# Respaced steps, a norm on another engine and a scheduling priority in a two-layer perceiver kernel

## The chip, the core and the metric

The kernel runs on one core of a Trainium2 chip. The metric is the device time of one launch in microseconds (us), as the median of repeated runs. The engines are named as the profile names them: PE (TensorE, matrix products), DVE (VectorE), ACT (ScalarE), POOL (GpSimd) and SP (SyncE, which issues most DMAs).

## The reference

The input is x, 64 sequences of 32 tokens with 256 features, and a context of 257 rows for each sequence. All is float32. There are two layers of three blocks, each added to x after a layer norm of x without weights:

```
x = x + cross_attn_0(context, norm(x), mask)   # 16 heads of 64; both sides layer-normed with g, b;
                                               # q and k rms-normed per head; keys = context + own tokens
x = x + self_attn_0(norm(x))                   # 16 heads of 16, q and k rms-normed
x = x + moe(norm(x))                           # 64 experts, top 8, 128 slots each, and a shared expert
x = x + cross_attn_1(norm(x), context)         # 16 heads of 64, plain softmax
x = x + self_attn_1(norm(x))                   # latent, rotary, causal
x = x + tanh((h W) A1 A2 + bias)               # h = norm(x)
```

The context's norm of the first block is the part that the change moves to another engine: `(cx - mean) * rstd * g + b` on 256 of the 257 rows of each context.

## The kernel before

**Tiles.** The 2048 tokens lie in 16 tiles `t` of 128 tokens; a tile holds four sequences, so there are 64 contexts `s = 4t + b`. The run has four stages: the first layer's cross-attention, with its self-attention and the routing threaded in (`before`); the experts (`experts`); the second layer (`after`); and drains in which the last tiles' steps run with nothing beside them.

**Who orders what.** PE executes exactly the order in which the Python code issues its instructions (`manual_schedule`). For all other engines a list scheduler orders the instructions: among those that it takes to be ready it picks the one with the lowest priority number, which is by default its place in the program. `nc.any` operations go to DVE or ACT as the scheduler chooses. PSUM has eight banks, all taken from one pool by `bank`.

**The first loop.** For each context `s` the body of the loop in `before` issues, in this order:

1. `keys(s+2)`: eight products `psA<-xT,wk` (L167, called at L195), their copies to `kT` by turns on ACT (L1201) and DVE (L1203), and after each four of them one squaring `sq` on ACT (L1206).
2. `weigh(s)`: the transposes of the attention weights (L207) and the copies `at` (L208).
3. slot 1.
4. `norms(s+2)`: eight small products of `sq` (L1218), `values(s)` (L221, L231, copies L233), `spread(s+2)` (L1239, exponentials L1240 on ACT).
5. slot 2.
6. `turn(s+3)` (transposes L1173, copy `xT` L1176), `scores(s+2)` (L1258, the multiplication L1267 out of PSUM on DVE, the softmax of L176 to L197 on DVE and ACT), `prepare(s+4)` (the context's norm).
7. slot 3, or, for the last context of a tile, the start of a tail.

A *slot* advances every live generator by one step, that is, up to its next `yield`. There are two kinds. A *front* is `CrossFirst.queries(t+1)`: norm, transposes, the query products, and the query transposes L1135. A *tail* is `tail(t)`: the output products (`heads_out`: `yT,wv`, then `wo,oT` at L258), the self-attention (`self_first`, `attend_self` with L310), and the routing (`route`). A tile has eleven slots, numbered i0 to i10 here: three in each context and two in the last. A `yield` with nothing before it moves later steps to later slots. So the placing of the yields decides which products of PE stand between a product of the main chain and the next one that needs its copy.

**The second loop.** In `after` the body is: `scores(s+2)`, slot A, `weigh(s)` (transposes L1375, copies `at` L1376), slot B, `values(s)`, slot C. The generators are `CrossSecond.queries(t+2)` and `follow(t)` (`heads_out`, `self_second`, `ffn`).

**The experts.** PE works through 64 experts, with the weights `we` fetched `AHEAD` = 12 experts ahead. After expert 12 `after_weights` loads and folds the second layer's weights; it ends with `latent_weights` and `ffn_weights`, whose scratch pools share memory.

Of the kernel before, what the change touches and what calls it, by code (L numbers as in the profile page):

```python
# [41 lines left out]
PLACES = (0, 2, 1, 3), (1, 3, 0, 2)  # L42

# [42 lines left out]

def done(steps):
    for _ in steps:
        pass


class Kernel:
# [7 lines left out]


# [50 lines left out]
    def normed(self, t):  # L152

        z = self.wk.tile([P, 1, D], F32, name="z")
        self.layernorm(z, self.x[:, t : t + 1, :])
        yield
        if self.slack:
            yield
        zT = self.wk.tile([P, 2, P], F32, name="zT")
        self.transposed(zT, z[:, 0, :])  # L160
        yield
        return z, zT
# [6 lines left out]
    def add_to_x(self, t, ps, bias=None):  # L169
        nc, xt = self.nc, self.x[:, t, :]  # L170
        if bias is not None:
            nc.gpsimd.tensor_tensor(xt, xt, bias, ALU.add)
        nc.vector.tensor_tensor(xt, xt, ps, ALU.add)
# [63 lines left out]
    def heads_out(self, t, yT, wv, wo, bias, split=False):  # L237
# [18 lines left out]
        yield  # L256
        ps = self.bank("psY")
        self.product(ps[:, :D], [oT[:, p, :] for p in range(8)], [wo[:, p, :] for p in range(8)])  # L258
        self.add_to_x(t, ps[:, :D], bias)
# [31 lines left out]
    def attend_self(self, t, e, recip, wo, bias):  # L291
# [6 lines left out]
        yield  # L298
        if self.slack:
            yield  # L300
# [71 lines left out]
    def before(self, ctx):  # L372


        self.eb, self.vb, self.slack = 1, 2, False
# [44 lines left out]
        next(first)  # L420
        next(first)
        cross.prepare(1)
        for i in range(2):
            cross.load(i + 2)
            cross.turn(i)
            cross.keys(i)
            cross.norms(i)
            done(first)
            cross.spread(i)
            cross.scores(i)  # L430
        cross.load(4)
        cross.prepare(2)
        cross.prepare(3)
        cross.turn(2)
# [47 lines left out]
        for s in range(n):  # L482
# [8 lines left out]
            if s + 2 < n:  # L491
                cross.keys(s + 2)
            cross.weigh(s)
            slot()
            if s + 2 < n:
                cross.norms(s + 2)
            cross.values(s)
            if s + 2 < n:
                cross.spread(s + 2)
            slot()  # L500
            if s + 3 < n:
                cross.turn(s + 3)
# [13 lines left out]
    def tail(self, t, yT, wv, wo, bo, sw, swo, sg, gw):  # L516

        yield from self.heads_out(t, yT, wv, wo, bo, True)
        yield
        if t == self.nt - 2:  # L520

            for _ in range(HOLD):
                yield
# [3 lines left out]
    def self_first(self, t, sw, swo, sg):  # L527
        nc = self.nc
        _, zT = yield from self.normed(t)
# [12 lines left out]
        )  # L542
        ps = self.bank("psA")
# [42 lines left out]
        yield from self.attend_self(t, e, recip, swo, None)  # L586

    def route(self, t, gw):
# [30 lines left out]

        yield  # L620
# [35 lines left out]
    def experts(self, ctx, slot, tails):  # L656
# [94 lines left out]
        for e in range(E):  # L751
# [8 lines left out]
            if e == AHEAD:  # L760
                self.after_weights()
        done(side)
# [34 lines left out]
    def after_weights(self):  # L797
# [8 lines left out]
        self.ffnw = self.ffn_weights(w)  # L806

    def after(self, ctx):
        self.eb = self.vb = 1
        self.slack = True  # L810
# [26 lines left out]
        for s in range(n):  # L837
# [3 lines left out]
            if s + 2 < n:  # L841
                cross.scores(s + 2)
# [5 lines left out]
            cross.weigh(s)  # L848
# [5 lines left out]
            cross.values(s)  # L854
# [115 lines left out]
    def self_second(self, t, wl, bl, wvo, bvo, wqk, bqk, wo, bo):  # L970
        nc = self.nc
        _, zT = yield from self.normed(t)
# [44 lines left out]
        yield  # L1017

# [25 lines left out]
        yield from self.attend_self(t, e, recip, wo, bo)  # L1044
# [18 lines left out]
    def ffn(self, t, m, bias):  # L1063
        nc = self.nc
        _, zT = yield from self.normed(t)
# [13 lines left out]
class CrossFirst:  # L1079
# [11 lines left out]
    def queries(self, t):  # L1091
# [8 lines left out]
        yield  # L1100
        lnT = k.wkx.tile([P, 2, P], F32, name="lnT")
# [7 lines left out]
        for n in range(2):  # L1109
# [10 lines left out]
            )  # L1120
        nc.vector.tensor_scalar(ss, ss, float(DH) * 1e-16, None, ALU.max)
# [34 lines left out]
    def prepare(self, s):  # L1156

        k, nc, cx = self.k, self.k.nc, self.cx[s]
        k.layernorm(cx, cx)
        nc.gpsimd.tensor_tensor(cx, cx, self.gx.unsqueeze(1).to_broadcast([P, 2, D]), ALU.mult)  # L1160
        nc.gpsimd.tensor_tensor(cx, cx, self.bx.unsqueeze(1).to_broadcast([P, 2, D]), ALU.add)
# [81 lines left out]
    def scores(self, s):  # L1243
# [6 lines left out]
        for half in range(2):  # L1250
# [14 lines left out]
            for i in range(2):  # L1265
                g = 2 * half + i
                nc.vector.tensor_tensor(sim[:, g, :], ps[i][:, :JK], sim[:, g, :], ALU.mult)  # L1267
# [18 lines left out]
class CrossSecond:  # L1286
# [7 lines left out]
    def queries(self, t):  # L1294

        k, nc = self.k, self.k.nc
        _, zT = yield from k.normed(t)
# [174 lines left out]
```

## Time and profile before

| | us |
|---|---|
| median of 3 runs | 2828.25 (2827.0 to 2829.42) |
| the profiled execution, own time | 2804.67 |
| its span, first to last instruction | 2802.8 |
| PE busy in the span | 2657.6 |
| DVE busy | 1694.9 |
| ACT busy | 1241.6 |
| POOL busy | 684.3 |

The profiled execution is 23.6 us (0.8%) under the median of the runs. A sum of durations from its trace is therefore set against its 2804.67 us, and carried over to the median in proportion.

How to read it: the end of a matrix product is modelled, so a product that waits in the middle of a group can look busy. In the timeline the first column is the start of a group and the second its modelled length. The distance from one group's start to the next group's start is what PE spent on the group, waits included. Groups of one kind are compared by that distance.

### The profile page before, as it was taken

What the parts mean: (1) busy time and instruction counts of PE and PEld (TensorE: products, weight loads), DVE (VectorE), ACT (ScalarE), POOL (GpSimd) and SP (SyncE); (2) the same over time, 40 slices, a digit from 0 to 9 for tenths busy, and PEclk for the clock granted to TensorE, in tenths of its full rate; (3) what the DMA queues carried; (4) which work ended last, traced back from release to release, by engine and by line L of the source; (5) the groups of instructions that cost most, each with busy time, mean ns of one, the idle gap of its engine ahead of it and who ended that gap; (6) DMA issues with size and microseconds to landing.
All of it is one profiled execution on the core that took longest, in us unless ns stands there. A gap on an engine that the chain in (4) does not pass through costs nothing. (4 is left out here: it accounts for less than half of the span.)

```text
span 2802.8 us, 58905 instructions
## 1 busy us (share of the span) xinstructions
PE 2657.6 (95%) x23386; PEld 1824.5 (65%) x23386; DVE 1694.9 (60%) x4427; ACT 1241.6 (44%) x3436; POOL 684.3 (24%) x756
## 2 busy tenths in 40 slices
PE   6999999999999999999999799999999999999996
PEld 3556666666666666666666578667777777777764
DVE  5546666666666666666665433466666666666664
ACT  3455555555555555555554223333333333333331
POOL 5211333133313331243121200321212222121001
PEclk8999999999999999999999899999999999999997
DMA  8000011011000000000001677321211222222110
GB/s 271 16 14 18 31 33 31 18 31 33 29 18 27 26 22 18 20 19 16 18 7 38 233 237 243 91 67 54 58 51 50 59 52 58 56 51 55 33 35 5
DMA packets 136087, 157.03 MB, mean 56 GB/s; under 512 B 24024, under 2 KB 118979, under 8 KB 135812
## 3 DMA queue, kind: packets, MB, share of 16 engines
q1 hardware_dynamic: 114308, 119.65, 13.8%
q0 software_dynamic: 12288, 25.21, 3.4%
q10 hardware_dynamic: 9216, 8.39, 0.9%
q8 instruction: 185, 3.03, 0.4%
q14 instruction: 90, 0.74, 0.1%
HBM read 121.63 MB, written 37.75 MB: 57 GB/s over the span
## 5 line engine op out<-in xcount | busy, mean ns | idle before, releaser
L167 PE MATMUL psA<-xT,wk 128*128 128x289 f32 x2048 | 517.4, 411 | 7.9 <-ACT xT L1176 4.5
L167 PEld LDWEIGHTS psA<-xT,wk 128*128 128x128 f32 x2048 | 388.0, 191 | 134.8 <-issue 21.8
L780 POOL DMA_INDIRECT y<-oute,idx x128 | 131.5, 1028 | 643.4 <-DVE x L791 453.9
L167 PE MATMUL psA<-at,cx 128*128 128x512 f32 x512 | 235.4, 602 | 20.0 <-ACT qTl L1005 18.2
L221 PE MATMUL psY<-at,cx 128*128 128x512 f32 x512 | 239.8, 612 | 0.1
L167 PE MATMUL psY<-xT,qk 128*128 128x257 f32 x1024 | 234.3, 382 | 0.0
L167 PEld LDWEIGHTS psY<-xT,qk 128*128 128x128 f32 x1024 | 190.8, 190 | 35.0 <-issue 10.2
L1357 DVE TENSOR_REDUCE mx<-psY 128x1 f32<-128x257 f32 x256 | 105.7, 423 | 133.6 <-PE psY L167 133.5
L1358 ACT ACTIVATE sim<-psY,mx 128x257 f32<-128x257 f32 x256 | 121.6, 476 | 142.3 <-DVE mx L1357 142.2
L184 ACT ACTIVATE sim<-sim,mx 128x289 f32<-128x289 f32 x256 | 134.1, 526 | 100.0 <-DVE mx L182 100.0
L221 PEld LDWEIGHTS psY<-at,cx 128*128 128x128 f32 x512 | 93.5, 192 | 123.0 <-issue 108.8
L167 PEld LDWEIGHTS psA<-at,cx 128*128 128x128 f32 x512 | 92.9, 190 | 120.8 <-issue 76.7
L233 ACT COPY yT<-psY 128x512 f32<-128x512 f32 x127 | 68.2, 589 | 220.7 <-PE psY L231 220.7
L645 POOL DMA_INDIRECT buf<-z,fi x128 | 126.5, 988 | 148.0 <-DVE fi L642 102.2
L1160 POOL TENSOR_TENSOR cx<-cx,a_gx 128x512 f32<-128x512 f32 x64 | 81.8, 1278 | 292.1 <-DVE cx L140 290.3
L1206 ACT ACTIVATE sq<-kT 128x1156 f32<-128x1156 f32 x128 | 149.4, 1167 | 4.4 <-DVE kT L1203 2.8
L1201 ACT COPY kT<-psA 128x289 f32<-128x289 f32 x256 | 94.8, 389 | 104.2 <-PE psA L167 104.2
L1376 ACT COPY at<-psT 128x512 f32<-128x512 f32 x145 | 78.8, 595 | 123.4 <-PE psT L1375 118.3
L1218 PE MATMUL psB<-sq,c 128*32 128x289 f32 x1024 | 109.4, 419 | 19.7 <-ACT sq L1206 19.5
L1388 DVE SCALAR_TENSOR_TENSOR yT<-at,xT,psA 128x512 f32<-128x512 f32 x128 | 94.0, 735 | 56.1 <-PE psA L167 50.7
L167 PE MATMUL psY<-yT,wv 128*64 128x128 f32 x2048 | 121.6, 275 | 1.6 <-DVE yT L1388 1.4
L1177 POOL COPY xT<-lnT 128x64 f32<-128x64 f32 x64 | 15.3, 240 | 423.0 <-PE psA L167 299.3
(257 smaller groups left out, 5190.5 us busy)
## 6 DMA issues: line engine op xcount, KB each, us to landing
cx<-in_ctx SPq DMA_DIRECT2D x128, 256.0 KB
we<-in_m_ew SPq DMA_DIRECT2D x64, 384.0 KB
xT<-in_ctxT SPq DMA_DIRECT2D x64, 257.0 KB
buf<-zero SPq DMA_DIRECT2D x32, 256.0 KB
be<-buf SPq DMA_DIRECT2D x64, 128.0 KB
oute<-oe ACTq DMA_DIRECT2D x64, 128.0 KB
mu<-in_mask SPq DMA_DIRECT2D x16, 128.5 KB
x<-in_x SPq DMA_DIRECT2D x16, 128.0 KB
```

Source lines behind the costliest of these rows:

```text
L167: self.nc.tensor.matmul(ps, lhsT=lhs[i], rhs=rhs[i], start=(i == 0), stop=(i == n - 1))
L184: nc.scalar.activation(sim[:, g, :], sim[:, g, :], AF.Exp, bias=mx[:, g : g + 1], accum_out=sm[:, g : g + 1])
L221: nc.tensor.matmul(ps[kc], lhsT=values[i][:, kc * P : (kc + 1) * P], rhs=at[i], start=(i == 0), stop=(i == n - 1 and tail is None),)
L645: d = nc.gpsimd.indirect_dma_start(out=self.buf[:, :], out_offset=bass.IndirectOffsetOnAxis(ap=fi[:, k : k + 1], axis=0), in_=z[:, 0, :], ...
L780: nc.gpsimd.indirect_dma_start(out=y, out_offset=None, in_=self.oute[:, :], in_offset=bass.IndirectOffsetOnAxis(ap=self.idx[:, t, k : k + ...
L1160: nc.gpsimd.tensor_tensor(cx, cx, self.gx.unsqueeze(1).to_broadcast([P, 2, D]), ALU.mult)
L1201: nc.scalar.copy(kT[:, p, :], ps[:, :JK])
L1206: nc.scalar.activation(sq[p // 4], kT[:, p - 3 : p + 1, :], AF.Square)
L1218: nc.tensor.matmul(ps[g * 32 : (g + 1) * 32, :JK], lhsT=k.pair[odd], rhs=sq[p // 4][:, p % 4, :], start=(odd == 0), stop=(odd == 1),)
L1357: nc.vector.tensor_reduce(mx[:, g : g + 1], ps[:, :J], AX.X, ALU.max, negate=True)
L1358: nc.scalar.activation(sim[:, g, :], ps[:, :J], AF.Exp, bias=mx[:, g : g + 1], accum_out=sm[:, g : g + 1])
L1388: nc.vector.scalar_tensor_tensor(self.yT[:, c, :, b * S : (b + 1) * S], self.at[:, 2, :].rearrange("p (h i) -> p h i", h=H), xT[:, c, J - ...
```

## The change

The change has seven parts.

- **Priority.** A context manager `urgent` lowers the priority number of what is issued in it by 400, in the order of one or two contexts' instructions. In the first loop it surrounds `keys`, `weigh`, `norms`, `values`, `spread`, `turn` and the multiplication L1267; in the second `weigh`, `scores` and `values`.
- **Spacing of the first loop's steps.** `attend_self` pauses for nine slots between the transposed weights and their product (two in the second layer, as many as before); `normed`, `self_first`, `route` and `queries` get further yields; `heads_out` does its last product in two halves of 128 columns, in two slots; the `HOLD` of the second last tail goes.
- **Context norm.** `prepare` does its affine part with four two-input operations of 256 elements on DVE, where two scalings on DVE and two 512-element operations on POOL stood.
- **Scores moved.** In the second loop `scores(s+2)` stands behind `weigh(s)` and no longer ahead of slot A.
- **Spacing of the second loop.** One more yield ahead of the self-attention's scores.
- **Feed-forward weights.** `ffn_weights` is called after expert 24 and not after expert 12.
- **Start.** The first two contexts' steps are interleaved, and contexts 2 to 4 are loaded before them.

```diff
+URGENT = 400
+def pause(n):
+    for _ in range(n):
+        yield
+    def urgent(self):
+        return self.tc.high_priority(offset=URGENT)
...
-    def normed(self, t):
+    def normed(self, t, steps=0):
         z = self.wk.tile([P, 1, D], F32, name="z")
         self.layernorm(z, self.x[:, t : t + 1, :])
         yield
-        if self.slack:
-            yield
+        yield from pause(steps)
...
-        ps = self.bank("psY")
-        self.product(ps[:, :D], [oT[:, p, :] for p in range(8)], [wo[:, p, :] for p in range(8)])
-        self.add_to_x(t, ps[:, :D], bias)
+        n = D // parts
+        for i in range(parts):
+            yield
+            cols = slice(i * n, (i + 1) * n)
+            ps = self.bank("psY")
+            self.product(ps[:, :n], [oT[:, p, :] for p in range(8)], [wo[:, p, cols] for p in range(8)])
+            self.add_to_x(t, ps[:, :n], bias[:, cols], cols)
...
         nc.vector.transpose(eT.rearrange("p a b -> p (a b)"), e.rearrange("p a b -> p (a b)"))
-        yield
-        if self.slack:
-            yield
+        yield from pause(steps)
...
         cross.prepare(1)
-        for i in range(2):
-            cross.load(i + 2)
-            cross.turn(i)
-            cross.keys(i)
-            cross.norms(i)
-            done(first)
-            cross.spread(i)
-            cross.scores(i)
-        cross.load(4)
+        for i in range(2, 5):
+            cross.load(i)
+        cross.turn(0)
+        cross.keys(0)
+        done(first)
+        cross.turn(1)
+        cross.norms(0)
         cross.prepare(2)
+        cross.spread(0)
+        cross.scores(0)
+        cross.keys(1)
+        cross.turn(2)
+        cross.norms(1)
         cross.prepare(3)
-        cross.turn(2)
+        cross.spread(1)
+        cross.scores(1)
...
             if s + 2 < n:
-                cross.keys(s + 2)
-            cross.weigh(s)
+                with self.urgent():
+                    cross.keys(s + 2)
+            with self.urgent():
+                cross.weigh(s)
             slot()
...
-        yield from self.heads_out(t, yT, wv, wo, bo, True)
-        yield
-        if t == self.nt - 2:
-            for _ in range(HOLD):
-                yield
+        yield from self.heads_out(t, yT, wv, wo, bo, True, 2)
+        yield
...
             if e == AHEAD:
                 self.after_weights()
+            if e == 2 * AHEAD:
+                self.ffnw = self.ffn_weights(self.w2)
...
-            if s + 2 < n:
-                cross.scores(s + 2)
             if b == NB - 2 and t + 2 < self.nt:
...
             slot()
-            cross.weigh(s)
+            with self.urgent():
+                cross.weigh(s)
+            if s + 2 < n:
+                with self.urgent():
+                    cross.scores(s + 2)
             slot()
...
     def prepare(self, s):
         k, nc, cx = self.k, self.k.nc, self.cx[s]
-        k.layernorm(cx, cx)
-        nc.gpsimd.tensor_tensor(cx, cx, self.gx.unsqueeze(1).to_broadcast([P, 2, D]), ALU.mult)
-        nc.gpsimd.tensor_tensor(cx, cx, self.bx.unsqueeze(1).to_broadcast([P, 2, D]), ALU.add)
+        mv, rs = k.stats(cx, 2)
+        for j in range(2):
+            x = cx[:, j, :]
+            nc.vector.scalar_tensor_tensor(x, x, mv[:, j, 0:1], self.gx, ALU.subtract, ALU.mult)
+            nc.vector.scalar_tensor_tensor(x, x, rs[:, j : j + 1], self.bx, ALU.mult, ALU.add)
...
-                nc.vector.tensor_tensor(sim[:, g, :], ps[i][:, :JK], sim[:, g, :], ALU.mult)
+                with k.urgent():
+                    nc.vector.tensor_tensor(sim[:, g, :], ps[i][:, :JK], sim[:, g, :], ALU.mult)
```

## The prediction, as put on record before the result

> **What bounds the kernel now.** I read the page's busy times first, then the windows by stage, PE's own waits, and last the timeline where PE waits.
>
> ```profile
> PE 2657.6 (95%) x23386; PEld 1824.5 (65%) x23386; DVE 1694.9 (60%) x4427; ACT 1241.6 (44%) x3436; POOL 684.3 (24%) x756
> PEclk8999999999999999999999899999999999999997
> ```
>
> PE is the bound, so only PE's lost time counts. By stage (columns: window, length, then busy time of PE, PEld, DVE, ACT and POOL, then the granted clock):
>
> ```profile
> 166.90:1466.40 1299.50, 1271.88 (x10884) 811.99 (x10880) 827.85 (x2322) 709.69 (x1919) 386.18 (x446) 1.00 0.08 23
> ...
> 1815.00:2686.00 871.00, 850.40 (x8381) 636.10 (x8378) 568.69 (x1326) 314.72 (x921) 180.75 (x173) 1.00 0.20 54
> ```
>
> The two steady loops seem to lose only 28 and 21 us. PE's own waits name what ends them:
>
> ```profile
> PE psB L1218 <- ACT sq L1206: 19.5, 23, 2.1
> PE psA L167 <- ACT qTl L1005: 18.2, 12, 1.7
> PE psY L310 <- DVE at L208: 14.7, 14, 1.3
> ```
>
> But a product that waits inside its group looks busy, so I go by starts. One context of the first loop:
>
> ```profile
> 776.44 1.47 PE L207 MATMUL psT<-c,sim 128*128 128x128 f32 x12
> 776.89 0.95 ACT L195 ACTIVATE sim<-sim,sm 128x289 f32<-128x289 f32 x2
> 777.75 0.68 ACT L1201 COPY kT<-psA 128x289 f32<-128x289 f32 x2
> 778.28 0.68 PE L1218 MATMUL psB<-sq,c 128*32 128x289 f32 x4
> 778.45 1.17 ACT L1206 ACTIVATE sq<-kT 128x1156 f32<-128x1156 f32 x1
> 779.67 1.17 PE L1218 MATMUL psB<-sq,c 128*32 128x289 f32 x12 [0.71 <-ACT sq L1206]
> 780.77 1.55 PE L221 MATMUL psY<-at,cx 128*128 128x512 f32 x3
> ```
>
> The last key products end at 776.44. ACT first scales an older softmax (L195), copies the keys at 777.75, squares at 778.45, and PE's norms (L1218) get their second half at 779.67. They take 780.77 - 778.28 = 2.49 us. With the output products of a tail in slot 1 they take 731.50 - 730.38 = 1.12:
>
> ```profile
> 726.69 3.77 PE L167 MATMUL psY<-yT,wv 128*64 128x128 f32 x64
> 730.38 1.19 PE L1218 MATMUL psB<-sq,c 128*32 128x289 f32 x16
> 731.50 3.70 PE L221 MATMUL psY<-at,cx 128*128 128x512 f32 x8
> ```
>
> **First loop, steady (tiles 1 to 14).** Start to start, the norms of a tile's other contexts take 1.78 (756.19), 2.49 and 1.79 (707.35) us: 0.66, 1.37 and 0.67 over 1.12. L310 takes 2.46 (704.89) in slot 1 of the last context against 1.22 in the second loop (2160.79): 1.24 over. Together 3.9 us of a tile's 93.5.
>
> In the new order slot 1 holds 3.7 us of output products at i0, half the query products at i3 and `self_first`'s q and k at i6 (four passes over 512 columns each, 1.7), and L310 and four transposes at i9 (1.22 + 0.53). From the end of the keys to the third norm product PE then has 1.35 + 1.7 + 0.3 = 3.3 us of work. The squares came 2.6, 3.2 and 4.8 us after the keys' end (the next group's start less the 0.84 that the rest of the norms takes), so spacing alone would leave 1.5 us at i9, most of it as the wait of L310. The priority puts copies (0.39) and square (1.17) ahead of L184 and L195, about 2 us after the keys' end, and frees banks for L310; its `eT` is nine slots old. I take 3.4 of the 3.9 as gained, the 0.5 going to what is late next: the query transposes L1135 now stand at i7, right ahead of the `scores` that need them, and their copy (0.59) has only `turn`'s 0.53 before it. 14 x 3.4 = 48 us; bounds 14 x 2.0 = 28 (spacing alone, less the 0.5) and 14 x 3.9 = 55.
>
> The other edits here cost PE nothing or little. **The norm**: 4 operations like L791 (0.478 us) for 2 like L140 (0.41) put 1.1 us a context on DVE, which has 828/56 = 14.8 of 23.2 us busy, and take 2 x 1.27 off POOL; `prepare` is two contexts ahead. DVE at 15.9 of 22.5 is the cover; without it, all 1.1 x 60 = 66 us. **The mask's** POOL work (L1147, 3.64 us) moves with L1135, but its reader is a softmax with two contexts to spare. **Longer tails** hold one-buffer tiles (`e`, `eT`, shared `q`/`oT`) for under eleven slots each: no wait. **The halved output product** is where a rule speaks against the change. In the trace
>
> ```profile
> 1590.42 1.06 PE L167 MATMUL psA<-beT,we 128*128 128x128 f32 x8
> 1591.31 0.60 PE L167 MATMUL psY<-we,eact 128*128 128x256 f32 x2
> ...
> 1591.96 1.89 PE L167 MATMUL psY<-sdn,act 128*128 128x256 f32 x8
> ```
>
> eight passes over 128 columns take 0.89 us from start to start and eight over 256 take 1.73 (the next group starts at 1593.69), 0.111 and 0.216 a pass: 32 x 0.111 against 16 x 0.216 is +0.1 us a tile, 1.5 in all. The Trainium skill ("TensorE: Matmul & The Clock Gate", Back-to-back issue gap) says that in a stream of weight loads and products the load counts too, so that 128 columns sustain one product in 81 ns where 56 would do. That factor of 1.45 would give 32 x 0.160 = 5.1 us and an estimate of +26 us. The row is of this chip and form: 1.5, inside the 0.5 above.
>
> **Start.** In tile 0 no tail covers ACT. Between 74 and 167 us the same excesses are L1218 0.5, 1.5, 1.7 and 2.9, transposes held up 2.1 (117.47), `xT` waits 0.8 and 1.9, and two groups of L221 that ran at half rate for 1.5 each (123.69, 147.39): 14 us. With ACT prompt I expect about 0.8 a context and no half rate on half the occasions: -8 (bounds -3 and -12). In the prelude (36 to 74 us) the waits are L1218 1.8 and 4.8, `nk` 0.8 and 0.6, `xT` 0.9 and 0.8, and 3 us of half rate. Interleaved, about 1.2 us stays before each `norms` and `spread`: -6 (-1 to -9).
>
> **Drain of the first loop.** The last tail's chain of norms, softmax and routing sets it, whatever the yields: 18 us of waits (L310 6.15, sel 2.74, z 2.39 and others) stay, with fewer products of tile 14 beside them and tile 13's instead. 0 (-4 to +4). The scatters (8 x 0.99 us on POOL) of three tails come in turn, as before.
>
> **Feed-forward weights.** The timeline has f_a issued at 1629.45, once the scratch of `latent_weights` was free, and PE waiting for it for 4.80 us; its sixteen passes then took 6.25 us (1633.27 to 1639.52) where 16 x 0.216 = 3.5. Twelve experts later (some 20 us) the data lies there, and the queue of SP only loses three issues ahead of `be`. -6.5; the lower end -3, if `be` (waits of 2.25 and 0.6 before) takes it back.
>
> **Start of the second layer.** PE waited 4.10 us at 1800.46 for tile 1's norm, behind `scores(2)` (3.5 us). Now `scores(2)` comes after that wait, which so grows to 7.6: +3.5; the wait of 1.16 at 1834.77 gets 3.5 us of cover and goes. +2 (0 to +4).
>
> **Second loop.** Where slot B is empty, `values` waits for `at`:
>
> ```profile
> 2191.29 1.47 PE L1375 MATMUL psT<-c,sim 128*128 128x128 f32 x12
> 2194.26 3.67 PE L167 MATMUL psA<-at,cx 128*128 128x512 f32 x8 [1.50 <-ACT qTl L1005]
> ```
>
> 2.97 from start to start, 1.31 elsewhere: 1.66 a tile. With `scores` between, it goes. But slots C and A now touch. Two pairs of steps lie across them, each a transposed norm and the product that reads it (C then A, in `self_second` and `queries`). A bare pair waits 0.46 at 1778.13, 0.6 from start to start. The second stands behind `qf` (0.75) and `kTl` (0.58): 0.9. So 1.5 a tile comes back: 14 x -0.2 = -3 (-12 to +8). **End drain**: one yield, no product moved: +1 (0 to +3).
>
> **Sum.** -48 - 8 - 6 + 0 - 6.5 + 2 - 3 + 1 = -68.5 against the profiled 2804.67, so 2736. The median is 0.8% higher: 2828.25 x 2736.2/2804.67 = 2759.
>
> **Rivals.** *Spacing helps, priority does not* (the scheduler's order hardly changes, or doesn't suit the chip): 1.4 us a tile stay, so 14 x 2.5 = 35 come in the steady loop and 5 of the start's 14: -35 - 5 - 6.5 + 2 - 3 + 1 = -46.5, 2781. For it: slot 1's cover alone explains the norms; against: L195 stands ahead of the copies in the timeline. *Waits return elsewhere* (L1135 to `scores`, and zT across C and A, each at twice my price): 14 x 0.5 + 14 x 1.5 = 28 of the 68.5 go, 2787. For it: the zT waits are sure, only their size is open; against: ACT is idle at those places now. *Slower: DVE blocks in order.* If DVE takes its queue strictly in turn, it stands still when an urgent copy is placed ahead of ready work and its product is not done. Over the keys (7.8 us of PE, four copies of 0.45 on DVE) that is up to 6.0 us a context, where DVE has 22.5 - 15.9 = 6.6 free. If `at`, `nk` and `yT` add 2, DVE needs 23.9 a context against 23.2 now: +42 us over 60 contexts, and -6.5 + 2 - 3 + 1: +35.5, 2864. It decides from 7.4 lost us a context. Against it: DVE takes the keys in bunches (L1203 waits 0.1 us a tile), and nothing in the trace shows it standing for long ahead of a copy. *That nothing changes* is out: PE's order is the program's, so the steps do move.
>
> **How the numbers follow.** The forecast, 2736 to 2775, gets 0.58; spacing alone 0.15 and waits elsewhere 0.14, both faster (2775 to 2810); slower 0.09; within 0.2% (5.7 us, about what measurement can tell from no change) 0.04, if the slower case is mild. The range runs from 2736, where most bounds fall well, to 2808. Faster 0.87, same 0.04, slower 0.09.
>
> **What would show it.** Right: L1218 start to start near 1.1 in all contexts, L310 1.2, no wait for f_a, a tile in 90 us, POOL near 520 us, and at each C and A a short wait for zT in the second loop. Wrong: L1218 still waiting for L1206, idle time on DVE before L1203 in microseconds, or a second-loop tile over 61.5 us.

## The result and the profile after

The changed kernel takes 2814.42 us (median of 5 runs, 2811.29 to 2815.95) beside 2828.25 us: a ratio of 0.9953, 95% interval 0.9942 to 0.9964, so 13.8 us or 0.47% faster. The forecast was 2759 us, range 2736 to 2808. The direction was right; a fifth of the gain came.

The profiled execution took 2814.6 us, like the timed ones. That of before (2804.67) had been 23.6 us under its timed runs, and this turns out to matter. First the page's busy times of after, then three windows, each from tile 0's output products to a later tile's: the first loop of before (14 tiles, first profile), the same loop of after, and the second loop of after (13 tiles). The columns are the length, the busy time of PE, PEld, DVE, ACT and POOL, and the granted clock.

```profile
PE 2650.2 (94%) x23642; PEld 1823.7 (65%) x23642; DVE 1730.6 (62%) x4544; ACT 1227.6 (44%) x3463; POOL 542.3 (19%) x644
```

```profile
165.94:1475.37 1309.43, 1281.81 (x10942) 820.05 (x10941) 836.57 (x2341) 716.07 (x1935) 388.72 (x448) 1.00 0.08 23
...
150.10:1462.28 1312.18, 1276.72 (x11023) 815.23 (x11022) 853.36 (x2395) 704.82 (x1954) 261.35 (x341) 1.00 0.08 22
1849.90:2652.90 803.00, 780.64 (x7820) 584.29 (x7818) 528.79 (x1222) 282.37 (x837) 164.23 (x159) 1.00 0.20 53
```

PE still bounds, at full clock. POOL lost 142 us of work (priced: 2 x 1.27 in 60 contexts, 152) and DVE took on 36. The norm's own operations on DVE grew as priced, from 66.0 to 132.6 us (priced: 66 more), so other work left DVE. With 853 of 1312 us it is no bound. But the 14 tiles of the first loop take as long as they did. PE's own waits in the steady part of the first loop say what changed:

```profile
PE psA L178 <- issue: 12.1, 28, 1.0
PE psB L1247 <- ACT sq L1235: 7.1, 11, 1.2
PE psT L161 <- issue: 3.9, 7, 1.1
PE psB L1287 <- ACT qTf L1167: 3.3, 13, 0.3
PE psB L1287 <- issue: 3.1, 10, 0.4
```

Line numbers of after are up to 30 higher: L178 is the product that was L167, L1247 the norms (L1218), L1287 the scores (L1258), L1235 the squaring (L1206), L665 the scatter (L645). The wait of L310 (13.7 us in before's first loop) is gone. What is new is "issue": PE stands, and the trace names nothing that it waits for. It happens once a tile, always at one place, where POOL issues the tile's eight *scatters*: indirect DMAs that write the rows of z to the experts' buffer. The timeline there, in one tile (PE's weight loads, SP and some small operations left out):

```profile
1398.55 1.08 POOL L665 DMA_INDIRECT buf<-z,fi  x1 [4.30 <-DVE fi L662]
...
1404.40 1.20 PE L1287 MATMUL psB<-kT,qTf 64*32 64x289 f32 x30
...
1405.91 0.67 PE L1287 MATMUL psB<-kT,qTf 64*32 64x289 f32 x2 [0.32 <-issue]
...
1406.51 0.33 PE L161 MATMUL psT<-c,z 128*128 128x128 f32 x1
1407.35 0.27 PE L161 MATMUL psT<-c,z 128*128 128x128 f32 x1 [0.51 <-issue]
1407.46 1.13 PE L178 MATMUL psA<-xT,wk 128*128 128x289 f32 x3
1407.60 0.98 POOL L665 DMA_INDIRECT buf<-z,fi  x1 [0.30 <-issue]
...
1408.81 0.89 PE L178 MATMUL psA<-xT,wk 128*128 128x289 f32 x3 [0.21 <-issue]
1410.24 6.50 PE L178 MATMUL psA<-xT,wk 128*128 128x289 f32 x26 [0.54 <-issue]
1410.29 1.56 DVE L1297 TENSOR_TENSOR sim<-psB,sim 128x289 f32<-128x289 f32 x4 [4.24 <-PE psA L178]
1410.57 0.37 ACT L162 COPY zT<-psT 128x256 f32<-128x256 f32 x1 [4.00 <-PE psA L178]
...
1421.02 1.17 PE L1247 MATMUL psB<-sq,c 128*32 128x289 f32 x12 [0.64 <-ACT sq L1235]
```

POOL issues eight scatters (1398.55 to 1408.58). From about 7 us after the first, DVE and ACT stand for 4 us although PE has finished what they are to take: the scores begun at 1404.40 are multiplied only from 1410.29 on, the transposes of z of 1407.35 are copied at 1410.57. PE itself goes on in steps of 0.7 or 1.4 us. All three are free some 1.7 us after the last scatter. It costs 3.0 us at once (scores 2.1 instead of 1.1 us from start to start, transposes 0.95 for 0.22, keys 9.1 for 7.8) and 1.3 more at the next norms, whose copies are late. Tiles 0 and 1, in which no scatter stands yet, last 90.16 and 89.12 us. Those after them last 94.1 to 94.5 (one 95.9); 94.2 below. The forecast had 90.

Two explanations fall by this trace alone. It is not the bytes: in the first tiles each scatter moves 128 KB, in the tile above all eight together 0.03 MB, and both tiles stall. The DMA row of the scatters, in the tile that begins them at 548.80 and in the one above (packets, MB, share of the DMA engines):

```profile
q0 software_dynamic: 384, 1.05, 16.6%
...
q0 software_dynamic: 384, 0.03, 2.1%
```

And it is not the loading of code: in three of the twelve tiles that stall (scatters from 548.80, 1115.87 and 1398.55 on) no packet of the instruction queues starts between 1 us before the first scatter and 16 us after it.

### The profile page after: what moved, and what is told of

Same layout as the page of the kernel before. It is cut to its first block, busy times and chain, and to the rows that moved or that the text cites. A ratio compares the mean times of both kernels' runs of the same rounds, so it can differ in the third digit from the quotient of the medians.

```text
span 2812.4 us, 59421 instructions
## 1 busy us (share of the span) xinstructions
PE 2650.2 (94%) x23642; PEld 1823.7 (65%) x23642; DVE 1730.6 (62%) x4544; ACT 1227.6 (44%) x3463; POOL 542.3 (19%) x644
## 5 line engine op out<-in xcount | busy, mean ns | idle before, releaser
L178 PE MATMUL psA<-xT,wk 128*128 128x289 f32 x2048 | 522.0, 410 | 17.9 <-issue 13.0
L178 PEld LDWEIGHTS psA<-xT,wk 128*128 128x128 f32 x2048 | 384.0, 190 | 150.1 <-issue 46.5
L178 PE MATMUL psA<-at,cx 128*128 128x512 f32 x512 | 233.5, 599 | 0.0
L178 PE MATMUL psY<-xT,qk 128*128 128x257 f32 x1024 | 233.5, 380 | 0.0
L178 PEld LDWEIGHTS psY<-xT,qk 128*128 128x128 f32 x1024 | 189.8, 190 | 25.1
L195 ACT ACTIVATE sim<-sim,mx 128x289 f32<-128x289 f32 x256 | 135.5, 532 | 64.4 <-DVE mx L193 64.3
L178 PEld LDWEIGHTS psA<-at,cx 128*128 128x128 f32 x512 | 93.4, 190 | 96.5 <-issue 83.3
L1235 ACT ACTIVATE sq<-kT 128x1156 f32<-128x1156 f32 x128 | 148.6, 1161 | 12.6 <-DVE kT L1232 11.4
L244 ACT COPY yT<-psY 128x512 f32<-128x512 f32 x128 | 68.7, 589 | 189.8 <-PE psY L242 189.8
L1297 DVE TENSOR_TENSOR sim<-psB,sim 128x289 f32<-128x289 f32 x256 | 100.7, 451 | 81.5 <-PE psA L178 37.9
L665 POOL DMA_INDIRECT buf<-z,fi x128 | 126.4, 987 | 96.3 <-DVE fi L662 54.0
L1232 DVE COPY kT<-psA 128x289 f32<-128x289 f32 x256 | 114.3, 451 | 40.0 <-PE psA L178 39.9
L178 PE MATMUL psY<-yT,wv 128*64 128x128 f32 x2048 | 127.9, 277 | 7.3 <-DVE yT L1418 7.3
L178 PEld LDWEIGHTS psY<-yT,wv 128*64 128x64 f32 x2048 | 116.6, 138 | 16.3 <-DVE yT L1418 11.2
L184 DVE TENSOR_TENSOR x<-x,psY 128x256 f32<-128x256 f32 (+1 forms) x80 | 29.2, 365 | 156.4 <-PE psY L178 154.8
L178 PE MATMUL psY<-wo,oT 128*128 128x128 f32 (+1 forms) x768 | 124.2, 315 | 0.0
```

The costliest lines, as they stand in the source:

```text
L178: self.nc.tensor.matmul(ps, lhsT=lhs[i], rhs=rhs[i], start=(i == 0), stop=(i == n - 1))
L195: nc.scalar.activation(sim[:, g, :], sim[:, g, :], AF.Exp, bias=mx[:, g : g + 1], accum_out=sm[:, g : g + 1])
L244: nc.any.tensor_copy(yT[:, kc, :, b * S : (b + 1) * S], ps[kc].rearrange("p (h i) -> p h i", h=H))
L665: d = nc.gpsimd.indirect_dma_start(out=self.buf[:, :], out_offset=bass.IndirectOffsetOnAxis(ap=fi[:, k : k + 1], axis=0), in_=z[:, 0, :], ...
L1232: nc.vector.tensor_copy(kT[:, p, :], ps[:, :JK])
L1235: nc.scalar.activation(sq[p // 4], kT[:, p - 3 : p + 1, :], AF.Square)
```

## The experiments

All ratios are to the kernel before on the same chip. Before itself took 2822 to 2825 us (medians) on three chips and 2800.2 on a fourth (runs of 2797 to 2803), where four of the kernels ran, as told there; so times from different chips are compared through before, or by stages. A tile's time is that of most tiles of the first loop from tile 2 on. Two theories at first. *Queue:* the small copies that complete `xT` stand behind the scatters on POOL (they end at 1408.94, PE's keys seem to follow). *Stutter:* the scatters hold up the other engines, whatever these wait for.

**A second profile of before.** No edit.

> The kernel before, unchanged, for a second profile. The first profiled execution took 2804.67 us, 23.6 us less than the median of its timed runs, and both theories below need to know where a typical execution spends these 23 us. Queue theory (the steady gain is lost because the two xT copies on POOL stand behind the 8 scatter transfers): a new profile shows no wait of the keys for POOL, since the scatters stand in slot 3 of context 0 and no xT copy follows within 7 us. Stutter theory (PE, and others with it, run slowly during the later part of every scatter, whatever they wait for): a typical execution shows 1.5 us or more lost in each of tiles 2 to 15 right beside the scatters, 20 us in all.

2822.08 us, ratio 0.9999 (0.9989 to 1.001), profiled execution 2826.98. The steady tile lasts 94.88 us where the first profile had 93.54. The timeline beside a scatter:

```profile
1045.02 3.70 PE L221 MATMUL psY<-at,cx 128*128 128x512 f32 x8
...
1047.83 0.97 POOL L645 DMA_INDIRECT buf<-z,fi  x1 [0.30 <-issue]
1048.65 1.13 PE L231 MATMUL psY<-at,c 64*128 64x512 f32 x4
...
1050.15 0.46 DVE L1226 TENSOR_SCALAR nk<-psB 128x289 f32<-128x289 f32 x1 [4.75 <-PE psY L231]
...
1050.64 0.45 ACT L1227 ACTIVATE nk<-nk 128x289 f32<-128x289 f32 x1 [5.69 <-DVE nk L1226]
...
1051.14 0.77 PE L1239 MATMUL psR<-nk,c 32*128 32x289 f32 x8 [1.36 <-ACT nk L1227]
```

The products of the norms were finished at 1045.02, and DVE takes them up at 1050.15. In the first profile, the same operation of the same program at the same place:

```profile
1038.65 3.70 PE L221 MATMUL psY<-at,cx 128*128 128x512 f32 x8
...
1038.94 0.45 DVE L1226 TENSOR_SCALAR nk<-psB 128x289 f32<-128x289 f32 x1
```

So this execution of before has the stall, and the one that I read had not, at the same pace of the scatters. The timed runs lie with this one. Between the two profiled executions are 22 us: 15 more in these 14 tiles (1324.5 against 1309.4 us), 9 more in the drain of the first loop (101.8 against 93.0), 2 less at the start. Most of the drain's 9 stands in one group, the 128 products of the last tile's L310, again beside scatters. In the first profile, then in this one:

```profile
1555.29 1.97 PE L310 MATMUL psY<-eT,vz 32*32 32x32 f32 x128 [6.15 <-DVE eT L297]
...
1570.42 0.68 PE L310 MATMUL psY<-eT,vz 32*32 32x32 f32 x41 [6.14 <-DVE eT L297]
...
1578.55 0.88 PE L310 MATMUL psY<-eT,vz 32*32 32x32 f32 x61 [1.09 <-issue]
```

In the loop before pays only 1.34 us a tile, because PE then has twelve products of `values` (L221, L231) before it that wait for nobody.

**The copies of `xT` off POOL.**

```diff
-        nc.gpsimd.tensor_copy(xT[:, :, J - 1 : JK - 1], lnT[:, :, b * S : (b + 1) * S])
-        nc.gpsimd.tensor_copy(xT[:, :, JK - 1 :], self.xlT[:, :, s : s + 1])
+        nc.vector.tensor_copy(xT[:, :, J - 1 : JK - 1], lnT[:, :, b * S : (b + 1) * S])
+        nc.vector.tensor_copy(xT[:, :, JK - 1 :], self.xlT[:, :, s : s + 1])
```

> The changed kernel with the two copies that complete xT (the 2x32 latent columns and the single last column) on VectorE instead of POOL, 60 contexts. Queue theory: the keys of context 1 slot 3 no longer wait 3 us behind the scatter, and the 1.3 us knock-on at the next norms goes too: 12 tiles x 4.3 = 50 us less, near 2765 us, tile period 90 us. Stutter theory: the 2 us lost at scores, z transposes and keys stay, the tile stays at 94 us, and the time at 2805 to 2815 us.

2812.8 us, 0.9957 (0.9942 to 0.9971): no gain, the tile lasts 93.8 us. The queue theory falls; that the keys followed POOL's copies was coincidence.

**The scatters one slot later.** In `route`, ahead of the placement product:

```diff
         yield
         yield
+        yield
```

> The changed kernel with a third yield in route ahead of the placement product and the 8 scatters, so that they stand in slot 3 of context 1 instead of slot 2, after the xT copies of that context instead of ahead of them. Queue theory: the same gain as with the copies on VectorE, about 50 us, near 2765 us. Stutter theory: PE is slowed for the same microseconds of a scatter wherever it stands, so 2805 to 2815 us.

2765.86 us, 0.9803 (0.9787 to 0.9819). Here I had the theories wrong: stutter as I wrote it (PE slowed wherever the scatter stands) forecast no gain, and 48 us came. Every steady tile now lasts 90.02 us. PE's waits from 240 to 1410 us are one row:

```profile
PE psB L1288 <- ACT qTf L1168: 3.4, 13, 0.3
```

Keys and scatters lie side by side as before, unharmed. Two things differ besides the place: the two POOL copies now fall between the first and the second scatter, and the fourth took 1.97 us instead of 0.97, so that the fifth starts 2.28 us after it, not 1.28. A *burst* theory: eight without a pause are too many. (Lines from `route` on are one higher here and below.)

```profile
1087.59 7.97 PE L178 MATMUL psA<-xT,wk 128*128 128x289 f32 x32
...
1090.50 1.97 POOL L666 DMA_INDIRECT buf<-z,fi  x1 [0.30 <-DVE kT L1233]
1092.78 0.97 POOL L666 DMA_INDIRECT buf<-z,fi  x1 [0.30 <-issue]
...
1098.52 1.18 PE L1248 MATMUL psB<-sq,c 128*32 128x289 f32 x16
```

**Both edits.** The later place, but with the copies on VectorE, so that nothing stands between the scatters.

> The changed kernel with both edits: the scatters one slot later and the two xT copies on VectorE, so that the 8 scatters of a tile go out back to back again (10.0 us, where the two copies and a wait between them had made it 11.2). Place theory (what matters is where in the context the scatter stands, since VectorE, ScalarE and PE then have other work in hand): stays fast, 2758 to 2770 us. Pace theory (eight scatters in 10.0 us are too many for something behind POOL, which then holds up all engines from about 7 us after the first to 1.5 us after the last; 11.2 us are not): the stalls come back, 2795 to 2820 us.

2831.4 us, 1.0019 (1.0009 to 1.0028). Each edit alone gained or was neutral; together they are 65 us slower than the later place alone: 59 in the loop (tiles of 92.1 to 96.7 us) and 7 in the end drain, at a granted clock of 0.71 there against 0.76. At the same slot the stall is back:

```profile
1122.99 1.07 POOL L666 DMA_INDIRECT buf<-z,fi  x1 [1.89 <-DVE junk L655]
...
1129.26 1.24 PE L178 MATMUL psA<-xT,wk 128*128 128x289 f32 x4 [0.94 <-issue]
...
1130.24 0.37 ACT L162 COPY zT<-psT 128x256 f32<-128x256 f32 x1 [6.60 <-remote]
...
1140.39 1.17 PE L1248 MATMUL psB<-sq,c 128*32 128x289 f32 x12 [2.03 <-ACT sq L1236]
```

So the place had not been the cure; the pauses between the scatters had.

**Half of the scatters left out.** `range(4)`, then `range(4, TOPK)`, at the changed kernel's own place; both leave half of the experts' rows unwritten.

> The changed kernel with scatters 5 to 8 of every tile left out (rows of the fifth to eighth choice are never written), at the old place. Pace theory: four in 5.1 us end before the stall begins at about 7 us, so the stall goes: 2755 to 2775 us. If the stall hangs on the first scatters' large transfers (130 and 119 KB, the last three move 1 to 2 KB each), it stays: 2800 to 2815 us. If POOL's queue alone counted, also near 2765, but the copies of xT on VectorE have already spoken against that.

> The changed kernel with scatters 1 to 4 of every tile left out (only the fifth to eighth choice's rows are written, nearly all of which fall away because their expert is full). Burst theory: four in a row do no harm whichever they are: 2748 to 2765 us. Rows theory (the stall comes from the late scatters, whose rows mostly lie out of bounds and move 1 to 2 KB): the stall stays, earlier: 2795 to 2815 us.

2752.11 us, 0.9736 (0.9719 to 0.9752), and 2753.14 us, 0.9756 (0.9737 to 0.9776): the tile lasts 90.02 us in both. Neither half does harm in the loop. The burst theory stands, the rows theory falls. (The expectation's 1 to 2 KB hold for late tiles only; in early ones the last four, too, move 128 KB each.) The drain of the first loop takes 103.2 and 101.1 us where after takes 112.5. There four in a row still cost a little: in last_four the 128 products of L322 take 3.5 us beside them (1478.02), with two gaps that the trace calls "issue", where 1.3 is the least.

**Even spacing.** After each scatter, in after and in before:

```diff
+            pad = self.small.tile([P, TOPK, 16], I32, name="pad")
+            nc.gpsimd.tensor_copy(pad, fi.unsqueeze(2).to_broadcast([P, TOPK, 16]))
```

> The changed kernel with a POOL copy of 128x128 numbers (about 0.3 us) after each scatter, so that eight of them take about 13 us instead of 10, at their old place in slot 2. Pace theory: no stall of PE, VectorE and ScalarE near the end of a scatter; the tile returns to 90 us and the time to 2760 to 2775 us, or less, since the drain's scatters are spaced too. Place theory: the xT copies of POOL now come 2 to 3 us later still, so the keys wait longer: 2815 to 2850 us.

> The kernel before with the same POOL copy after each scatter. Pace theory: a typical execution loses its 1.3 us beside each scatter and up to 8 us in the drain no longer: 2795 to 2808 us, near the first profiled execution (2804.67). Place theory: 2820 to 2830 us, no change.

2802.56 us, 0.9921 (0.9903 to 0.9939), and 2817.95 us, 0.997 (0.9959 to 0.9981). Between the theories: it comes to 1.45 us from scatter to scatter and 11.3 for eight, where I had expected 13. In after the "issue" gaps of PE are gone, but ACT still stands until 11.3 us after the first scatter, the norms wait 1.9 us a tile for `sq`, and the tiles last 92.1 to 95.6 us. In before the tile lasts 93.83 us, so most of its 1.34 is back; its drain (102.6) is not. The 11.2 us of scatter_later, with gaps after the first and the fourth, had cost nothing. So it isn't the mean pace alone.

**A gap in the middle.** First by a yield between the fourth and fifth scatter, in before, and in after with the third yield:

```diff
         for k in range(TOPK):
+            if k == TOPK // 2:
+                yield
             d = nc.gpsimd.indirect_dma_start(
```

> The kernel before with a yield in the middle of the scatters and nothing else. Burst theory: a typical execution gets back about 1.3 us a tile and the drain's stall of 7 us: 2793 to 2806 us instead of 2822 to 2825, so that the change would be worth 45 us or so between two kernels that both are free of the stall. If the stall in before has another cause: 2818 to 2828 us.

> The changed kernel with the third yield ahead of the placement product and one more yield in the middle of the scatters, so that four go out in slot 3 of context 1 and four in slot 1 of context 2, and also in the drain. Burst theory (only a burst of more than four scatters without a pause holds the engines up): no stall in the loop (tile 90 us), and none in the two drains where scatter_later still lost about 6 us each: 2750 to 2762 us. If the drain's stalls are hidden by the tails' own chain anyway: 2763 to 2770 us, as scatter_later (2765.86).

Before: 2810.21 us, 0.9953 (0.9936 to 0.9969); starts 3.1 us apart in the middle, the steady tile at 93.55 us: its stall is gone. The drain is as long as in the second profile (102.5 us): a yield orders the program, it doesn't hold POOL, which there issues up to eight in a row. For that reason the forecast for the drain missed, and 2767.25 us, 0.98 (0.9784 to 0.9816), is no better than the third yield alone.

The trace of split_later holds a test that nobody planned. In ten of its twelve later tiles the fourth scatter takes 1.8 to 2.0 us and the fifth starts 2.1 to 2.3 us after it, as in scatter_later; those tiles last 90.02 us. In the other two it takes 0.97 and the fifth follows after 1.28; those last 95.01 and 92.83. The fourth scatter in a tile of each kind:

```profile
639.60 1.95 POOL L668 DMA_INDIRECT buf<-z,fi  x1 [0.30 <-DVE kT L1235]
...
729.61 0.97 POOL L668 DMA_INDIRECT buf<-z,fi  x1 [0.30 <-issue]
```

The pause after the first scatter (1.62 us from start to start) stands in all twelve. So it is the one after the fourth that goes with the cure, and nothing in the program asks for it.

Then by a POOL copy, without and with the third yield:

```diff
+            if k == TOPK // 2:
+                pad = self.small.tile([P, TOPK, 128], I32, name="pad", bufs=1)
+                nc.gpsimd.tensor_copy(pad, fi.unsqueeze(2).to_broadcast([P, TOPK, 128]))
```

> The changed kernel with one POOL copy of 128x1024 numbers (about 2 us) between the fourth and the fifth scatter, everything at its old place. Burst theory (eight without a pause hold the engines, two bursts of four do not): no stall; the tile near 90 to 91 us and the time 2755 to 2775 us, with the xT copies on POOL 2 us later and perhaps 1 us of wait of the keys for them. If only the slot matters: 2800 to 2820 us.

> The changed kernel with the third yield ahead of the scatters and the same POOL copy between the fourth and the fifth. Burst theory: the loop as with the third yield alone (90 us a tile), and the drain's two stalls of some 6 us gone as well: 2752 to 2762 us. If the drain's stalls lie beside a chain that ends last anyway: 2763 to 2770 us.

2755.94 us, 0.9842 (0.9827 to 0.9857), and 2767.01 us, 0.988 (0.9864 to 0.9895). The copy took 1.1 us, not the 2 expected, so that the fifth scatter starts 2.19 us after the fourth. These ran on the chip where before took 2800.2, so they prove less than they seem. The tile lasts 90.02 us in both, but after without the pause never ran there, and the stall is mild on that chip. L322 in the drain beside eight scatters in a row shows it, first in scatter_later, then in later_second_before (below), which has the same first layer and ran on this chip:

```profile
1454.19 0.51 PE L322 MATMUL psY<-eT,vz 32*32 32x32 f32 x33
...
1460.88 1.08 PE L322 MATMUL psY<-eT,vz 32*32 32x32 f32 x78 [0.50 <-issue]
...
1455.46 2.19 PE L322 MATMUL psY<-eT,vz 32*32 32x32 f32 x128
```

The 128 products take 7.76 us there and 2.19 here. So the pause had little to take away, and with the third yield it lengthens the tails' chain: the drain takes 113.3 us in later_pause and 108.8 in later_second_before.

**Without the priority.** `URGENT = 0`; PE's order stays the same.

> The changed kernel with the priority offset at 0: PE's order stays, the orders of VectorE, ScalarE and POOL fall back to the scheduler's own. If priority carries the short norms (1.1 us in every context), they go back to 1.8 to 2.5 in the contexts whose slot 1 holds little, some 1 to 1.5 us a tile, 15 to 20 us slower than the changed kernel: 2830 to 2835 us. If spacing alone carries them, within 5 us of 2814. If the priority itself does harm by taking VectorE or POOL from what is due, faster than 2810.

2835.68 us, 1.004 (1.0028 to 1.0051): against the changed kernel's 0.9953 and 0.9962 the priority is worth 0.8 to 0.9%, some 23 us: 7 in the second loop (809.9 us against 803.0), 8 up to tile 0's output products (157.7 against 150.1), 4 at the end (64.4 against 60.3) and only 4 in the 14 tiles of the first loop (1316.3 against 1312.2). The norms' wait for `sq` there is 17.7 us against 7.1, but both kernels have the stall. What the priority is worth in this loop without it was not run.

**The second loop.** First its order alone back, still with the priority and the added yield:

```diff
+            if s + 2 < n:
+                with self.urgent():
+                    cross.scores(s + 2)
             slot()
             with self.urgent():
                 cross.weigh(s)
-            if s + 2 < n:
-                with self.urgent():
-                    cross.scores(s + 2)
             slot()
```

> The kernel with the split scatters, and the second loop's products in the order of before (scores ahead of slot A, not between A and B). By the profile of the changed kernel the new order saved 1.66 us a tile at values and lost 0.6 and 0.9 at the two normed tiles and 0.85 at the output products: 0.4 to 0.5 us a tile should come back, 4 to 8 us less than the kernel with split scatters alone, so 2744 to 2757 us. If instead the loss is the longer steps (yields) and not the order: no difference beyond 3 us, or slower by up to 12.

2784.4 us, 0.9868 (0.9851 to 0.9884): 17 us slower than split_later, not 4 to 8 faster. The loop takes 816.9 us instead of 804.6; the end takes 68.7 instead of 60.0, at a granted clock of 0.68 there against 0.76, which I can't account for. PE's waits in the loop are nearly all in one row:

```profile
PE psA L178 <- ACT sim L1391: 25.4, 13, 2.1
```

The move of the scores is right, given the priority and the added yield. Then order, priority and yield all as before, on top of the third yield, and of both the third yield and the pause:

```diff
+            if s + 2 < n:
+                cross.scores(s + 2)
...
-            with self.urgent():
-                cross.weigh(s)
-            if s + 2 < n:
-                with self.urgent():
-                    cross.scores(s + 2)
+            cross.weigh(s)
...
-            with self.urgent():
-                cross.values(s)
+            cross.values(s)
...
         nc.any.tensor_copy(kT, ps)
         yield
-        yield
```

> The changed kernel with the third yield, and the whole second loop as before: scores ahead of slot A, no priority, one yield less in self_second. If the loop's edits cost what the stages show (803 to 805 us against 796.4, and 60.0 against 57.1 at the end): 2752 to 2760 us. If the loss comes from the first layer's side (buffers, weights loaded at another time) and not from the loop's edits: 2763 to 2770 us.

> Third yield, the POOL copy between the fourth and the fifth scatter, and the second loop as before. The two savings should add: 2742 to 2754 us, about 1.023 to 1.027 times as fast as the changed kernel as it stands.

2750.54 us, 0.9825 (0.981 to 0.984), and 2755.85 us, 0.9845 (0.9831 to 0.9858); against later_pause on the same chip the old second loop gives 11 us (796.1 us against 804.5 in thirteen tiles, 57.4 against 59.9 at the end, 70.2 against 71.9 at the start). The pause adds 5 us here, where no stall is left in the loop for it to take away. The 2750.54 is the lowest time of a kernel that does all the work, but on the chip where before, too, is fastest; the ratio of scatter_later (0.9803) is lower.

**The last pair.** The changed kernel once more, and the pause in place with the old second loop.

> The changed kernel, unchanged, on one chip with the kernel before and the last version. If the stall is as on the first chips: 2812 to 2816 us beside 2820 to 2828 for before. If the chip is one where before takes about 2800, the changed kernel's stall is either still there (2805 to 2815 us, a change that slows on such a chip), or as mild as before's (2780 to 2795 us).

> The changed kernel with the POOL copy between the fourth and the fifth scatter at their own place, and the second loop as before. The two savings add: 2755.94 with the pause alone, less 10 to 11 for the second loop (later_pause 2767.01 against pause_second_before 2755.85): 2743 to 2748 us. If the tails' end and the second loop overlap in what they save: 2750 to 2756 us.

2812.48 us, 0.9962 (0.9948 to 0.9975), and 2773.63 us, 0.9819 (0.9806 to 0.9833), on a chip where before takes 2823.94. The forecast of 2743 to 2748 missed: the stall is shorter with the pause, but not gone. On this chip the tile lasts 94.2 us in after and 91.5 with the pause, and in the drain L322 beside the scatters takes 9.0 and 7.3. So the pause does cure part of the stall with the scatters at their own place, but a fifth scatter 2.19 us after the fourth instead of 1.28 isn't enough to cure it all.

## Why the prediction was wrong

By stages, in us, against the first profile of before (itself without the stall). The right column is scatter_later, the change without the stall in its loop:

| stage | forecast | after | scatter_later |
|---|---|---|---|
| start, with tile 0's contexts | -14 | -15.8 | -15.5 |
| first loop, 14 tiles | -48 | +2.8 | -49.9 |
| drain of the first loop | 0 | +19.5 | +19.3 |
| experts (feed-forward weights) | -6.5 | -6.9 | -7.3 |
| start of the second layer | +2 | +1.1 | +1.0 |
| second loop to its last tile | -3 | +6.0 | +7.6 |
| end drain | +1 | +3.0 | +2.7 |
| sum | -68.5 | +9.7 | -42.1 |

Against the second profile of before, which has the stall, after gains 12.3 us in the first loop and loses 10.7 in its drain. That is 36 and 11 us short of the forecast; the second loop and the end are 11 short. These make up nearly all that is missing.

**The step that failed** is "The scatters (8 x 0.99 us on POOL) of three tails come in turn, as before". `route` was moved from slot 3 of context 0 to slot 2 of context 1, and I costed its eight DMAs only as POOL time in the drain. They hold up DVE, ACT and PE from some 6 to 12 us after the first of them. At the old place PE then had products of `values` that need nothing fresh, and the stall cost 1.34 us a tile. At the new place it has scores, a transposed norm and keys, each needing a copy by DVE or ACT or the bank that one frees, and it costs 4.2 us (94.2 against 90.02). That undoes the whole 3.52 us gained.

**The mechanism of the first loop** was right, to 0.1 us, once the pauses between the scatters are there: 93.54 to 90.02 a tile is 3.52, the forecast 3.4. In after the norms take 1.11 us from start to start in three contexts of four, and 1.22 is all that L322 (before L310) takes. The query copy `qTf` takes 0.3 us a tile back, less than the 0.5. The halves of the output product take 1.84 and 1.89 us where the whole took 3.51: +0.2 us a tile, near the +0.1 of the row shown and far from the +1.6 of the factor that was set aside. How the 3.52 divides between spacing and priority was not run.

**The step to the median** was wrong in the same way. I scaled by 0.8%, as if the 23.6 us were a uniform slowness. By before_again they lie in the loop (15 us) and in the drain (9), where the scatters are. The trace that I argued from was of an execution that lacked the very effect that decides, and I had no reason for the gap. It may have run on a chip like the fourth; on which it ran isn't recorded.

**The drain** was costed at nothing, "with fewer products of tile 14 beside them". It grew by 19.5 us. With half of the scatters left out it takes 103.2 and 101.1 us, against 93.0 in the first profile and 112.5 in after: 8 to 10 us stay with the longer tails, of which more is left when the loop ends, and about as much goes with the scatters. Pause_in_place agrees: on the chip with the mild stall, with all eight scatters, its drain takes 102.4 us. PE's part of the stall, in the drain of after, is a row of single 32x32 products with gaps for which the trace names nothing:

```profile
1541.68 0.54 PE L322 MATMUL psY<-eT,vz 32*32 32x32 f32 x38
...
1543.91 0.18 PE L322 MATMUL psY<-eT,vz 32*32 32x32 f32 x1 [1.23 <-issue]
...
1544.65 0.21 PE L322 MATMUL psY<-eT,vz 32*32 32x32 f32 x1 [0.55 <-issue]
1545.36 0.26 PE L322 MATMUL psY<-eT,vz 32*32 32x32 f32 x2 [0.51 <-issue]
...
1548.25 1.12 PE L322 MATMUL psY<-eT,vz 32*32 32x32 f32 x82 [1.16 <-issue]
```

**The second loop.** The two transposed norms take 0.6 and 0.9 us a tile more from start to start, as priced (the trace's waits for them: 25, 14.8 us in twelve tiles), and `values` no longer waits. What I did not see is a third wait, of the output products for `yT`, which take 4.54 us from start to start for 3.69:

```profile
PE psA L178 <- ACT zT L162: 14.8, 25, 0.7
PE psY L178 <- DVE yT L1418: 5.5, 12, 0.5
```

A tile went from 61.54 to 61.97 us, not to 61.3, and the last is 1.7 to 3.4 us longer. As a whole this part of the change loses 11 us (pause_second_before against later_pause). Which of order and yield does it stays open: going back on the order alone made it worse, and the priority helps in the new order (no_priority).

**Start, weights and VectorE** held within 2 us: no wait for `f_a` remains, and no wait of PE names the norm on DVE. **The rivals:** that the priority does nothing falls by no_priority, which is 23 us slower than after and slower than before. Of "DVE blocks in order" the sign came, and not the cost: DVE now stands ahead of the key copies, some 3 us a tile, and PE waits for none of it. In scatter_later, from 240 to 1410 us:

```profile
DVE kT L1233 <- PE psA L178: 38.7, 39, 1.5
```

"Waits return elsewhere" was right for the second loop only. None of them had the scatters. One slip among the sums changes nothing here: the rival of spacing alone counts 14 x 2.5 = 35 us in the first loop and leaves out the 0.5 that the bounds take off (14 x 2.0 = 28).

Open: what holds the engines (only when, how long and in which pattern is shown); why the fourth scatter is drawn out in scatter_later; why one chip, and one first profile, hardly show the stall; and the fastest kernel on a chip that stalls, since the third yield with the old second loop ran only on the mild one.

## What to carry to other kernels

When a step is moved, list its DMAs with it, and ask what the other engines are doing from the first to some microseconds after the last; a burst of transfers does least harm beside products that need no fresh copy. If the profiled execution lies off the timed runs by more than their spread, find out where before the sum is made: a second profile of the same kernel would have shown the stall. And test the cure at a second place: that the third yield gained 48 us was luck, for a reason that had nothing to do with its purpose.

## What the hardware showed that was not expected

Eight indirect DMAs issued by POOL 1.28 us apart can hold up PE, DVE and ACT together, from 5 to 7.5 us after the first until 1.3 to 1.7 us after the last. PE then goes on in steps of 0.7 and 1.4 us. It happens with 1.05 MB in the eight as with 0.03 MB. In the loop four of them in a row did not (90.02 us a tile with either half), and eight with a gap after the fourth held the engines less or not at all (2.2 to 3.1 us from start to start there, 0 to 1.5 us a tile). It does not happen in every execution: beside the same burst the same 128 products took 9.0 us in one profile of before and 1.97 in another, and 7.76 us on one chip and 2.19 on another. The trace calls it "issue" or "remote", or blames an engine that was done long before; a wait of 4 to 7 us on two engines that ends at one moment is the sign to look for.
